# An attention and dynamic-filter kernel: score tiles of one and three banks in attention, and layer 1 without its split taps

## The chip, the cores and the metric

The kernel runs on one core of a Trainium2 chip. A core has five engines with instruction streams of their own: TensorE (PE, matmuls), VectorE (DVE), ScalarE (ACT), GpSimd (POOL) and SyncE (SP), and queues for transfers (DMA). They wait for each other through semaphores. The metric is the device time of one execution in microseconds. For the kernel before, it is the median of three runs.

## The reference, cut to what matters

Two layers work on `x` of shape (4, 256, 48, 48) in fp32. Layer 0 is a 3x3 convolution, then attention over all 2304 pixels with 8 heads of 32 channels. Layer 1 makes 45 weights for each pixel and uses them as five 3x3 filters with dilations 1, 6, 12, 24 and 36.

```python
# layer 0, after the convolution, its norm and relu
qkv = jnp.einsum('oc,bchw->bohw', qkv_w, x) + qkv_b[None, :, None, None]
q, k, v = (qkv[:, :, :d], qkv[:, :, d:2 * d], qkv[:, :, 2 * d:])      # per head, d = 32
attn = jax.nn.softmax(jnp.einsum('bhdn,bhdm->bhnm', q, k) * scale, axis=-1)
out = jnp.einsum('bhem,bhnm->bhen', v, attn).reshape(B, C, H, W)
out = jnp.einsum('oc,bchw->bohw', proj_w, out) + proj_b[None, :, None, None]
# layer 1
guidance = _conv(x, W_cat, pad=1)                                     # 45 channels
outs = [x]
for i, d in enumerate((1, 6, 12, 24, 36)):
    w = jax.nn.softmax(guidance[:, 9 * i:9 * (i + 1)], axis=1)
    outs.append(_dyn_branch(x, w, d))       # sum over 9 taps: shifted x times w[:, k]
y = _conv(jnp.concatenate(outs, axis=1), W_scale, pad=0)              # then a batch norm
# both layers: x = x + layer(group_norm(x))
```

## The kernel before

The images go through the core one after the other. Attention of image `b` stands alone. After it, layer 1 of image `b` runs together with the convolution and the q, k, v projections of image `b + 1`; after the last image, layer 1 stands alone, and the output is written.

**Attention.** The 2304 query columns of a group of four heads (there are two groups) are cut into units of 512 columns; eight units hold one group each, a ninth holds the last 256 columns of both. A unit goes through 18 key blocks `m` of 128 keys. A step is one block of one unit: four score matmuls, one for each head on its own 32 rows of the array, the exponential on ScalarE, then four matmuls that add the weighted values into `num`, and the sum of the exponentials over blocks (the divisor) on VectorE in `acc`. The order in the program is: scores of step i, then the weighted sums of step i - 1. PSUM has eight banks of 512 fp32 columns; three tiles of two banks hold scores, one bank holds `num`, one `den`.

```python
QC = 512
LENT = (2, 5, 8, 11, 14)
...
def ps2(name):
    return ps_s.tile([P, 2, 512], F32, tag="s", name=name)         # bufs=3

def scores(u, m):
    ss = [ps2(f"se_{b}_{u}_{m}_{pair}") for pair in range(2)]
    for g, q0, n, at in units[u]:
        for j, r in enumerate(heads):
            nc.tensor.matmul(ss[j // 2][:, j % 2, at : at + n],
                             k_[r, g, m * P : (m + 1) * P], q[r, g, q0 : q0 + n], ...)
    p = work0.tile([P, 4, QC], F32, tag="p", name=f"p_{b}_{u}_{m}", bufs=4)
    for pair in range(2):
        nc.scalar.activation(p[:, 2 * pair : 2 * pair + 2, :], ss[pair], AF.Exp, scale=QS)
    return p
```

For the five blocks in `LENT`, VectorE adds two of the four heads only; the other two are added by a transfer from GpSimd's queue that sums into `extra` in SBUF. After the last block `num` is copied out by ScalarE, so that its bank is free. `close` makes the divisor of a unit: it sums `acc` (and first `extra`) over the keys by a matmul with ones, takes the reciprocal by way of two transposes, and multiplies. `project` applies the output projection to 384 finished columns.

```python
def weigh(u, m, p):
    ...                                    # four matmuls p x vT into num
    if m == NT - 1:
        nc.vector.tensor_tensor(st["acc"][:, 2:], st["acc"][:, 2:], extra, ALU.add)
    ...
    js = slice(0, 2 if m in LENT else 4)
    nc.vector.tensor_tensor(st["acc"][:, js], other[:, js], p[:, js], ALU.add)
    if m == LENT[0]:
        nc.gpsimd.dma_start(out=extra, in_=p[:, 2:])
    elif m in LENT:
        nc.gpsimd.dma_start(out=extra, in_=p[:, 2:], accum_op=ALU.add)
    ...
    elif m == NT - 1:
        st["out"] = out
        nc.scalar.copy(out, st["num"])

for i, (u, m) in enumerate(steps):
    ps = scores(u, m)
    if prev is not None:
        weigh(*steps[i - 1], prev)
    prev = ps
    if m == 2 and u:
        close(u - 1)
    if m == 6 and u % NH == 0:
        ...                                # project finished chunks, in a ps2 tile
    if m > 2 and u > 1 and spare:
        spare.pop(0)(ps_a)                 # pieces of the next image's normalization
```

**Layer 1.** For each tap, a matmul (or a transfer and a copy) spreads the weight of a pixel over 128 partitions (`wb`), VectorE multiplies it with the shifted image, and GpSimd adds the product into `cat`; the sums then go through the output matmuls (`py`). The program's order is decided as it is built: a `clock` with estimated durations of each engine says which matmuls of layer 1 and of the next image's convolution come when. Some taps of the last image skip GpSimd: their products go straight into matmuls (`single`). Where GpSimd is behind by more than `SPLIT` on that clock, a tap in the first ones of a filter is split: VectorE multiplies both halves and adds one of them, and GpSimd adds only the other.

```python
split = (at > 0 and mine and not single
         and clock.t["POOL"] + added > clock.t["DVE"] + SPLIT)
mine = at == 0 or split or (mine and single)
...
elif split:
    nc.vector.tensor_tensor(pv, pw, src[:, 0], ALU.mult)
    nc.vector.tensor_tensor(pw, pw, src[:, 1], ALU.mult)
    dst = catv[:, 1, l0:l1, x0:x1]
    nc.vector.tensor_tensor(dst, dst, pw, ALU.add)
    dst = catv[:, 0, l0:l1, x0:x1]
    nc.gpsimd.tensor_tensor(dst, dst, pv, ALU.add)
```

Of the kernel before, what the change touches and what calls it, by code (L numbers as in the profile page):

```python
# [32 lines left out]

QC = 512
SAFE = 60.0
LENT = (2, 5, 8, 11, 14)
CATS = 4
PRODS = 5
SLACK = 3000.0
SPLIT = 4500.0  # L40
BEHIND = 0.0


# [5 lines left out]
def conv_preact_kernel(  # L49
# [482 lines left out]
    with tc.tile_pool(name="w", bufs=1) as wpool, tc.tile_pool(  # L532
# [394 lines left out]
        def attention(b, q, k_, vT, pools, spare, project, scratch):  # L927
# [6 lines left out]
            out = scratch[:, :QC]  # L934

            extra = scratch[:, QC : 3 * QC].rearrange("p (j n) -> p j n", j=2)
# [5 lines left out]
            assert NH * rest == QC  # L942
            heads = [slice(j * D, (j + 1) * D) for j in range(4)]

            def ps2(name):
                return ps_s.tile([P, 2, 512], F32, tag="s", name=name)

            def scores(u, m):
                ss = [ps2(f"se_{b}_{u}_{m}_{pair}") for pair in range(2)]
                for g, q0, n, at in units[u]:  # L950
                    for j, r in enumerate(heads):
                        nc.tensor.matmul(  # L952
                            ss[j // 2][:, j % 2, at : at + n],
                            k_[r, g, m * P : (m + 1) * P],
                            q[r, g, q0 : q0 + n],
                            start=True,
                            stop=True,
                        )
                p = work0.tile([P, 4, QC], F32, tag="p", name=f"p_{b}_{u}_{m}", bufs=4)
                for pair in range(2):  # L960
                    nc.scalar.activation(  # L961
                        p[:, 2 * pair : 2 * pair + 2, :], ss[pair], AF.Exp, scale=QS
                    )
                return p

            state = {}

            def weigh(u, m, p):
                if m == 0:
                    state[u] = dict(  # L970
                        num=ps_a.tile([P, 512], F32, tag="num", name=f"num_{b}_{u}"),
                        acc=work0.tile([P, 4, QC], F32, tag="acc", name=f"acc_{b}_{u}"),
                    )
                st = state[u]
                several = len(units[u]) > 1
                if several and m == 0:

                    for j, r in enumerate(heads):
                        nc.tensor.matmul(st["num"][r, :], zeros, p[:, j, :], start=True, stop=False)
                for i, (g, q0, n, at) in enumerate(units[u]):  # L980
                    for j, r in enumerate(heads):
                        nc.tensor.matmul(  # L982
                            st["num"][r, at : at + n],
                            vT[:, m, g * P + j * D : g * P + (j + 1) * D],
                            p[:, j, at : at + n],
                            start=(m == 0 and not several),
                            stop=(m == NT - 1 and i == len(units[u]) - 1),
                        )
                end = u == len(units) - 1
                if m == NT - 1:  # L990
                    nc.vector.tensor_tensor(st["acc"][:, 2:], st["acc"][:, 2:], extra, ALU.add)
                if end and m == NT - 1:
                    sums(u, p, True, False)
                elif m == 0:
                    st["first"] = p
                else:
                    other = st["first"] if m == 1 else st["acc"]
# [3 lines that stand above are left out]
                        nc.gpsimd.dma_start(out=extra, in_=p[:, 2:])  # L1001
                    elif m in LENT:
                        nc.gpsimd.dma_start(out=extra, in_=p[:, 2:], accum_op=ALU.add)  # L1003
                if end:
                    st["out"] = st["num"]
                elif m == NT - 1:
                    st["out"] = out
                    nc.scalar.copy(out, st["num"])  # L1008

            def sums(u, rhs, start, stop):  # L1010
                if start:
                    state[u]["den"] = ps_a.tile([P, 512], F32, tag="den", name=f"den_{b}_{u}")
                for j, r in enumerate(heads):
                    nc.tensor.matmul(
                        state[u]["den"][r, :], ones, rhs[:, j, :], start=start, stop=stop
# [1 line left out]

            def close(u):

                sums(u, state[u]["acc"], u < len(units) - 1, True)  # L1020
                st = state.pop(u)
                t = scratch
                nc.vector.transpose(t, st["den"])
# [4 lines left out]
                    rc.unsqueeze(2).to_broadcast([P, QC // D, D]),  # L1028
                )
                for g, q0, n, at in units[u]:  # L1030
                    nc.vector.tensor_tensor(
                        ao[:, g, q0 : q0 + n], st["out"][:, at : at + n], t[:, at : at + n],
                        ALU.mult,
                    )

            steps = [(u, m) for u in range(len(units)) for m in range(NT)]
            prev = None
            chunk = 0
            for i, (u, m) in enumerate(steps):
                ps = scores(u, m)  # L1040
                if prev is not None:
                    weigh(*steps[i - 1], prev)
                prev = ps
                if m == 2 and u:
                    close(u - 1)
                if m == 6 and u % NH == 0:
                    while (chunk + 1) * CH <= units[u][0][1]:
                        project(chunk, ao, ps2(f"pp_{b}_{chunk}"))
                        chunk += 1
                if m > 2 and u > 1 and spare:  # L1050
                    spare.pop(0)(ps_a)
            while spare:
                spare.pop(0)(ps_a)
            weigh(*steps[-1], prev)
            close(len(units) - 1)
            return ao, chunk

        def project(b, c, ao, pp, norm):
# [42 lines left out]
        def dynamic_filters(b, ao, chunk, norm, other, pools):  # L1101
# [241 lines left out]
            for c in range(NCK):  # L1343
# [21 lines left out]
                for j, (n, at, (k, oy, ox, y0, y1, x0, x1)) in enumerate(taps):  # L1365
# [18 lines left out]
                    else:  # L1384
# [25 lines left out]
                    split = (  # L1410
                        at > 0 and mine and not single
                        and clock.t["POOL"] + added > clock.t["DVE"] + SPLIT
                    )
                    mine = at == 0 or split or (mine and single)
                    if at == 0:
                        nc.vector.tensor_tensor(catv, wb, src, ALU.mult)  # L1416
                        end = summed = clock("DVE", ns, given)
                    elif split:
                        prod = work1.tile(
                            [P, NH, CH], F32, tag="prod", name=f"prod_{b}_{c}_{k}", bufs=PRODS  # L1420
                        )
                        pv = prod[:, 0, : nr * ncol].rearrange("p (r w) -> p r w", w=ncol)
                        pw = wb[:, 0]
                        nc.vector.tensor_tensor(pv, pw, src[:, 0], ALU.mult)
                        first = clock("DVE", half, given, slot("prod", PRODS))
                        nc.vector.tensor_tensor(pw, pw, src[:, 1], ALU.mult)
                        dst = catv[:, 1, l0:l1, x0:x1]
                        nc.vector.tensor_tensor(dst, dst, pw, ALU.add)
                        end = clock("DVE", 2 * half)
                        dst = catv[:, 0, l0:l1, x0:x1]  # L1430
                        nc.gpsimd.tensor_tensor(dst, dst, pv, ALU.add)
                        summed = max(clock("POOL", added / 2 + 90, first), end)
                        free["prod"].append(clock.t["POOL"])
                    else:
                        if single:
                            mixed("single", 2 * NH)
# [10 lines left out]
                    if single:  # L1447
                        for o in range(NH):
# [8 lines left out]
                    elif at and not split:  # L1457
                        dst = catv[:, :, l0:l1, x0:x1]
                        nc.gpsimd.tensor_tensor(dst, dst, pv, ALU.add)  # L1459
                        summed = clock("POOL", added, end)  # L1460
# [108 lines left out]
        for b in range(B + 1):  # L1569
# [130 lines left out]
            if b + 1 < B:  # L1700
# [1 line left out]
                u_next = taken(ORDER[0])  # L1702
                fin = [None]

                def step(ps_a, nn=nn, fin=fin, b=b):
                    if fin[0] is None:
                        fin[0] = nn.finish(
                            lambda name: ps_a.tile([P, 512], F32, tag="den", name=name)
                        )
                    if next(fin[0], fin) is fin:  # L1710
                        nn.shift_of()

                def piece(h, r0, b=b, nn=nn):
                    t = inside(pads[(b + 1) % 2], h, r0, R)
                    return lambda ps_a: nc.scalar.activation(
                        t, t, AF.Identity, bias=nn.shift[:, h : h + 1], scale=nn.rstd[:, h : h + 1]
                    )

# [3 lines left out]
            norm1 = Norm("n1", b)  # L1722
            q, k_, vT = qkv[b]
            with tc.tile_pool(name=f"work0_{b}", bufs=2) as work0, tc.tile_pool(
                name=f"ps_s_{b}", bufs=3, space=PSUM
            ) as ps_s, tc.tile_pool(name=f"ps_a_{b}", bufs=1, space=PSUM) as ps_a:
                ao, chunk = attention(
                    b, q, k_, vT, (ps_s, ps_a, work0), [f for _, f in spare],
# [77 lines left out]
```

## Time and profile before

| What | Value |
|---|---|
| median of three runs | 2929.42 us |
| range of the runs | 2926.9 to 2933.61 us |
| span of the profiled execution | 2927.6 us |
| mean granted clock of TensorE | 0.982 |
| exponentials (ScalarE) | 1296, mean 1027 ns, 1260.0 us |
| score matmuls, weighted sums (instructions) | 5760 and 5760 |
| adds into `acc` (VectorE) | 572, mean 1955 ns |
| summing transfers (GpSimd's queue) | 180, 4.5 us from issue to landing |
| adds into `cat` (GpSimd), whole and half | 661 and 81 |

The profile gives the busy time of each engine, groups of instructions by program line (with busy time, mean duration, and the idle time just before them with what ended it), and a timeline. Each fp32 matmul of the program appears as two instructions. A share of busy time says what an engine does, and not what it waits for: a PE whose matmul has begun and waits in the middle of a group counts as busy. So the stages have to be looked at apart, and within a stage, the steps.

### The profile page before, as it was taken

The page shows a single profiled execution, that of the slowest core. Times are in us where ns is not written, and L with a number is a line of the kernel's source. Part 1 is how long each engine was busy: PE and PEld are TensorE (multiplying, and loading weights), DVE is VectorE, ACT ScalarE, POOL GpSimd, SP SyncE. Part 2 cuts the span into 40 slices and gives each one's busy share as a digit, 9 for nine tenths or more (in the row PEclk, how much of TensorE's full clock was granted, in tenths as well). Part 3 has the DMA queues.
Part 4 walks back from the last instruction along what each step waited for, and adds up shares of the span by engine and source line. Part 5 has one row for each costly group of instructions (what it writes and reads, how often), then busy time and mean ns, then how long its engine had stood idle before and what let it go on. Part 6 is the DMA issues. An engine that isn't in the chain of part 4 may idle for free. (4 is left out here: it accounts for less than half of the span.)

```text
span 2927.6 us, 43833 instructions
## 1 busy us (share of the span) xinstructions
PE 2773.1 (95%) x16950; PEld 1246.7 (43%) x16950; DVE 2426.1 (83%) x2574; ACT 1675.2 (57%) x2104; POOL 1205.2 (41%) x1024
## 2 busy tenths in 40 slices
PE   7999999999999999999899999999999999998994
PEld 5622223556542222456562222355555222244562
DVE  6388999789868899778986899978886999986886
ACT  3489888322348988712236988852233888871224
POOL 1010010898840010299791100059986010005894
PEclk9999999999999999999999999999999999998997
DMA  4432333132252233323225333322213333335225
GB/s 179 100 69 64 67 76 71 53 87 86 73 127 62 61 78 69 68 65 95 69 68 124 71 69 69 68 63 76 82 50 85 69 75 67 71 67 218 54 74 204
DMA packets 146233, 244.64 MB, mean 84 GB/s; under 512 B 60952, under 2 KB 111968, under 8 KB 144224
## 3 DMA queue, kind: packets, MB, share of 16 engines
q0 software_dynamic: 26720, 99.79, 15.4%
q1 hardware_dynamic: 76960, 87.31, 10.4%
q10 hardware_dynamic: 42336, 54.66, 7.2%
q8 instruction: 135, 2.21, 0.3%
q14 instruction: 82, 0.67, 0.1%
HBM read 115.02 MB, written 32.33 MB: 50 GB/s over the span
## 5 line engine op out<-in xcount | busy, mean ns | idle before, releaser
L961 ACT ACTIVATE p<-se 128x1024 f32<-128x1024 f32 x1296 | 1260.0, 1027 | 239.7 <-PE se L952 171.2
L999 DVE TENSOR_TENSOR acc<-acc,p 128x2048 f32<-128x2048 f32 (+1 forms) x572 | 1118.4, 1955 | 101.2 <-ACT p L961 55.0
L1459 POOL TENSOR_TENSOR cat<-cat,prod 128x752 f32<-128x752 f32 (+9 forms) x661 | 883.1, 1345 | 133.6 <-DVE prod L1442 96.7
L952 PE MATMUL se<-q,k 32*128 32x512 f32 (+1 forms) x5760 | 819.6, 596 | 12.5 <-ACT p L961 6.2
L982 PE MATMUL num<-p,vT 128*32 128x512 f32 (+1 forms) x5760 | 699.0, 565 | 9.0 <-ACT scratch L1008 7.4
L1442 DVE TENSOR_TENSOR prod<-wb,pad 128x384 f32<-128x384 f32 (+8 forms) x687 | 483.4, 738 | 94.4 <-POOL cat L1459 55.9
L952 PEld LDWEIGHTS se<-q,k 32*128 32x128 f32 x5760 | 299.2, 184 | 533.6 <-issue 368.5
L1003 POOL DMA_DIRECT2D scratch<-p x144 | 122.6, 852 | 922.1 <-ACT p L961 872.9
L1281 PE MATMUL py<-cat,wsc 128*128 128x384 f32 x960 | 349.9, 494 | 9.8 <-POOL cat L1459 8.3
L1382 ACT COPY wb<-ws 128x384 f32<-128x384 f32 (+3 forms) x260 | 121.7, 468 | 371.1 <-DVE prod L1442 237.0
L982 PEld LDWEIGHTS num<-p,vT 128*32 128x32 f32 x5760 | 122.3, 108 | 491.2 <-issue 443.0
L1385 PE MATMUL wb<-w,pick 128*128 128x384 f32 (+3 forms) x628 | 299.7, 509 | 24.7 <-DVE prod L1442 15.8
L1281 PEld LDWEIGHTS py<-cat,wsc 128*128 128x128 f32 x960 | 176.3, 192 | 114.8 <-POOL cat L1459 24.8
L1001 POOL DMA_DIRECT2D scratch<-p x36 | 20.1, 558 | 467.8 <-DVE acc L999 339.2
L1385 PEld LDWEIGHTS wb<-w,pick 128*128 128x128 f32 x628 | 116.5, 190 | 140.2 <-DVE prod L1442 63.4
L851 PE MATMUL pc<-cv_q,u 128*128 128x288 f32 x576 | 160.9, 413 | 7.0 <-DVE cv_q L742 6.2
L1133 PE MATMUL pg<-pad,wcat 128*45 128x384 f32 x864 | 158.4, 498 | 1.6 <-DVE pad L592 1.4
L851 PE MATMUL pc<-cv_k,u 128*128 128x288 f32 x576 | 155.0, 407 | 3.3 <-DVE yt L786 1.8
L884 PE MATMUL pq<-hid,wqkv 128*128 128x384 f32 x384 | 135.5, 492 | 11.8 <-DVE yt L786 11.8
L851 PEld LDWEIGHTS pc<-cv_q,u 128*128 128x128 f32 x576 | 108.3, 192 | 37.3 <-DVE cv_q L742 6.3
L1416 DVE TENSOR_TENSOR cat<-wb,pad 128x768 f32<-128x768 f32 x120 | 114.0, 950 | 11.4 <-PE wb L1385 10.8
L851 PEld LDWEIGHTS pc<-cv_k,u 128*128 128x128 f32 x576 | 106.6, 189 | 32.5 <-DVE yt L786 2.5
(221 smaller groups left out, 1976.4 us busy)
## 6 DMA issues: line engine op xcount, KB each, us to landing
scratch<-p POOLq DMA_DIRECT2D x180, 512.0 KB, 4.5
ws<-w_d ACTq DMA_DIRECT2D x256, 192.0 KB, 3.2
pad<-in_x SPq DMA_DIRECT2D x14, 1152.0 KB, 15.6
u<-u_d SPq DMA_DIRECT2D x18, 768.0 KB, 4.7
x_d<-pad SPq DMA_DIRECT2D x48, 192.0 KB, 2.5
xst<-in_x SPq DMA_DIRECT2D x36, 192.0 KB, 2.4
y_d<-y SPq DMA_DIRECT2D x18, 384.0 KB, 3.4
u_d<-u SPq DMA_DIRECT2D x6, 768.0 KB, 3.7
```

The lines of the kernel that those rows point to most:

```text
L851: nc.tensor.matmul(m, u[:, h, kx, o * P : (o + 1) * P], halves[g][:, h, i, :, kx : kx + WW], start=(h == 0 and kx == 0), stop=(h == NH - 1 ...
L884: nc.tensor.matmul(pq[:, :CH], wqkv[:, i, s, g * P : (g + 1) * P], hid[:, i, cols], start=(i == 0), stop=(i == NH - 1),)
L952: nc.tensor.matmul(ss[j // 2][:, j % 2, at : at + n], k_[r, g, m * P : (m + 1) * P], q[r, g, q0 : q0 + n], start=True, stop=True,)
L961: nc.scalar.activation(p[:, 2 * pair : 2 * pair + 2, :], ss[pair], AF.Exp, scale=QS)
L982: nc.tensor.matmul(st["num"][r, at : at + n], vT[:, m, g * P + j * D : g * P + (j + 1) * D], p[:, j, at : at + n], start=(m == 0 and not s ...
L999: nc.vector.tensor_tensor(st["acc"][:, js], other[:, js], p[:, js], ALU.add)
L1003: nc.gpsimd.dma_start(out=extra, in_=p[:, 2:], accum_op=ALU.add)
L1133: nc.tensor.matmul(pg[64 * s : 64 * s + NG, :CH], wcat[:, ii, k, :], window(gn, ii, cc * R, k // 3 - 1, k % 3 - 1), start=(i == 0 and k == 0),
L1281: nc.tensor.matmul(to, wsc[:, n * NH + i, o * P : (o + 1) * P], rhs(i), start=(n == 0 and i == 0), stop=(last and i == NH - 1),)
L1385: nc.tensor.matmul(pw[:, : nr * WW], pick[:, k : k + 1].to_broadcast([P, P]), w[:, l0 * WW : l1 * WW], start=True, stop=True,)
L1442: nc.vector.tensor_tensor(pv, wb, src, ALU.mult)
L1459: nc.gpsimd.tensor_tensor(dst, dst, pv, ALU.add)
```

## The change

In attention:

- Scores of head 0 go into a tile of one bank (one buffer), those of heads 1 to 3 into a tile of three banks (two buffers). With `num`, these are all eight banks. The exponential is taken in 512 and 1536 columns. The aim is that the scores of a step need not wait for the exponentials of the step just before.
- The bank for `den` is gone. The divisor of a unit takes its turn among the three-bank tiles, as do the projection and the statistics of the next image's norm. It is made two units later, ahead of the weighted sums, so that a turn of the tiles comes where PE has other work.
- Six key blocks are summed by transfers instead of five. The sum with `extra` comes after the unit's last add. `num` is copied straight into `ao`, where it is multiplied in place.

In layer 1 the split taps are gone, and with them `SPLIT`; the estimated duration of GpSimd's adds for 36 columns and fewer is 110 ns shorter than in the kernel before.

The diff, cut to its core:

```diff
-LENT = (2, 5, 8, 11, 14)
+LENT = (2, 5, 8, 10, 13, 15)
-SPLIT = 4500.0
...
-            def ps2(name):
-                return ps_s.tile([P, 2, 512], F32, tag="s", name=name)
+            def three(name):
+                return ps_s.tile([P, 3, 512], F32, tag="s", name=name)     # bufs=2

             def scores(u, m):
-                ss = [ps2(f"se_{b}_{u}_{m}_{pair}") for pair in range(2)]
+                s1, s3 = ps_a.tile([P, 512], F32, tag="one", ...), three(f"se_{b}_{u}_{m}")
...
+                        dst = s3[:, j - 1] if j else s1
...
-                for pair in range(2):
-                    nc.scalar.activation(
-                        p[:, 2 * pair : 2 * pair + 2, :], ss[pair], AF.Exp, scale=QS
-                    )
+                nc.scalar.activation(p[:, 0, :], s1, AF.Exp, scale=QS)
+                nc.scalar.activation(p[:, 1:, :], s3, AF.Exp, scale=QS)
...
-                if m == NT - 1:
-                    nc.vector.tensor_tensor(st["acc"][:, 2:], st["acc"][:, 2:], extra, ALU.add)
...
+                if m == NT - 1:
+                    rest = st["acc"][:, 2:]
+                    nc.vector.tensor_tensor(rest, rest, extra, ALU.add)
+                    if not end:
+                        g, q0, n, _ = units[u][0]
+                        nc.scalar.copy(ao[:, g, q0 : q0 + n], st["num"])
...
-                    state[u]["den"] = ps_a.tile([P, 512], F32, tag="den", name=f"den_{b}_{u}")
+                    state[u]["den"] = three(f"den_{b}_{u}")[:, 0, :]
...
                 ps = scores(u, m)
+                if m == 1 and u > 1:
+                    close(u - 2)
                 if prev is not None:
                     weigh(*steps[i - 1], prev)
                 prev = ps
-                if m == 2 and u:
+                if m == 2 and u == last:
                     close(u - 1)
-                if m == 6 and u % NH == 0:
-                    while (chunk + 1) * CH <= units[u][0][1]:
-                        project(chunk, ao, ps2(f"pp_{b}_{chunk}"))
+                if m == 6 and (u % NH == 1 or u == last):
+                    while (chunk + 1) * CH <= units[u if u == last else u - 1][0][1]:
+                        project(chunk, ao, three(f"pp_{b}_{chunk}"))
...
-                    half = 0.525 * ns + 150
-                    ns, added = 1.05 * ns + 150, 2.1 * ns + (80 if 36 < ncol < WW else 190)
+                    ns, added = 1.05 * ns + 150, 2.1 * ns + (190 if ncol == WW else 80)
...
-                    split = (
-                        at > 0 and mine and not single
-                        and clock.t["POOL"] + added > clock.t["DVE"] + SPLIT
-                    )
-                    mine = at == 0 or split or (mine and single)
...                  (the split branch, shown above, is taken out)
```

More of the change, by code (lines that the diff above doesn't have):

```diff
@@ L933, in attention @@
             nc.gpsimd.memset(zeros, 0.0)
-            out = scratch[:, :QC]
-            extra = scratch[:, QC : 3 * QC].rearrange("p (j n) -> p j n", j=2)
+            extra = scratch[:, : 2 * QC].rearrange("p (j n) -> p j n", j=2)
             scratch = work0.tile([P, QC], F32, tag="rt", name=f"rt_{b}", bufs=1)
@@ L943, in attention @@
             heads = [slice(j * D, (j + 1) * D) for j in range(4)]
-            def ps2(name):
-                return ps_s.tile([P, 2, 512], F32, tag="s", name=name)
+            def three(name):
+                return ps_s.tile([P, 3, 512], F32, tag="s", name=name)
             def scores(u, m):
-                ss = [ps2(f"se_{b}_{u}_{m}_{pair}") for pair in range(2)]
+                s1, s3 = ps_a.tile([P, 512], F32, tag="one", name=f"so_{b}_{u}_{m}"), three(f"se_{b}_{u}_{m}")
                 for g, q0, n, at in units[u]:
                     for j, r in enumerate(heads):
+                        dst = s3[:, j - 1] if j else s1
                         nc.tensor.matmul(
-                            ss[j // 2][:, j % 2, at : at + n],
+                            dst[:, at : at + n],
                             k_[r, g, m * P : (m + 1) * P],
@@ L959, in scores @@
                 p = work0.tile([P, 4, QC], F32, tag="p", name=f"p_{b}_{u}_{m}", bufs=4)
-                for pair in range(2):
-                    nc.scalar.activation(
-                        p[:, 2 * pair : 2 * pair + 2, :], ss[pair], AF.Exp, scale=QS
-                    )
+                nc.scalar.activation(p[:, 0, :], s1, AF.Exp, scale=QS)
+                nc.scalar.activation(p[:, 1:, :], s3, AF.Exp, scale=QS)
                 return p
             state = {}
+            last = len(units) - 1
             def weigh(u, m, p):
@@ L988, in weigh @@
                         )
-                end = u == len(units) - 1
-                if m == NT - 1:
-                    nc.vector.tensor_tensor(st["acc"][:, 2:], st["acc"][:, 2:], extra, ALU.add)
+                end = u == last
                 if end and m == NT - 1:
@@ L1003, in weigh @@
                         nc.gpsimd.dma_start(out=extra, in_=p[:, 2:], accum_op=ALU.add)
[L1004 to L1008, printed above, removed]
+                if m == NT - 1:
[4 more added lines that the diff above has]
+                        nc.scalar.copy(ao[:, g, q0 : q0 + n], st["num"])
             def sums(u, rhs, start, stop):
                 if start:
-                    state[u]["den"] = ps_a.tile([P, 512], F32, tag="den", name=f"den_{b}_{u}")
+                    state[u]["den"] = three(f"den_{b}_{u}")[:, 0, :]
                 for j, r in enumerate(heads):
@@ L1018, in close @@
             def close(u):
-                sums(u, state[u]["acc"], u < len(units) - 1, True)
+                sums(u, state[u]["acc"], u < last, True)
                 st = state.pop(u)
@@ L1030, in close @@
                 for g, q0, n, at in units[u]:
-                    nc.vector.tensor_tensor(
-                        ao[:, g, q0 : q0 + n], st["out"][:, at : at + n], t[:, at : at + n],
-                        ALU.mult,
-                    )
+                    dst = ao[:, g, q0 : q0 + n]
+                    src = dst if u < last else st["num"][:, at : at + n]
+                    nc.vector.tensor_tensor(dst, src, t[:, at : at + n], ALU.mult)
             steps = [(u, m) for u in range(len(units)) for m in range(NT)]
@@ L1043, in attention @@
                 prev = ps
-                if m == 2 and u:
+                if m == 2 and u == last:
                     close(u - 1)
-                if m == 6 and u % NH == 0:
-                    while (chunk + 1) * CH <= units[u][0][1]:
-                        project(chunk, ao, ps2(f"pp_{b}_{chunk}"))
+                if m == 6 and (u % NH == 1 or u == last):
+                    while (chunk + 1) * CH <= units[u if u == last else u - 1][0][1]:
+                        project(chunk, ao, three(f"pp_{b}_{chunk}"))
                         chunk += 1
                 if m > 2 and u > 1 and spare:
-                    spare.pop(0)(ps_a)
+                    spare.pop(0)(three)
             while spare:
-                spare.pop(0)(ps_a)
+                spare.pop(0)(three)
             weigh(*steps[-1], prev)
-            close(len(units) - 1)
+            close(last)
             return ao, chunk
@@ L1407, in dynamic_filters @@
                     )
-                    split = (
-                        at > 0 and mine and not single
-                        and clock.t["POOL"] + added > clock.t["DVE"] + SPLIT
-                    )
-                    mine = at == 0 or split or (mine and single)
                     if at == 0:
@@ L1417, in dynamic_filters @@
                         end = summed = clock("DVE", ns, given)
[L1418 to L1433, printed above, removed]
                     else:
@@ L1456, in dynamic_filters @@
                             ))
-                    elif at and not split:
+                    elif at:
                         dst = catv[:, :, l0:l1, x0:x1]
@@ L1703, in conv_preact_kernel, with step @@
                 fin = [None]
-                def step(ps_a, nn=nn, fin=fin, b=b):
+                def step(three, nn=nn, fin=fin, b=b):
                     if fin[0] is None:
-                        fin[0] = nn.finish(
-                            lambda name: ps_a.tile([P, 512], F32, tag="den", name=name)
-                        )
+                        fin[0] = nn.finish(lambda name: three(name)[:, 0, :])
                     if next(fin[0], fin) is fin:
@@ L1714, in piece @@
                     t = inside(pads[(b + 1) % 2], h, r0, R)
-                    return lambda ps_a: nc.scalar.activation(
+                    return lambda three: nc.scalar.activation(
                         t, t, AF.Identity, bias=nn.shift[:, h : h + 1], scale=nn.rstd[:, h : h + 1]
@@ L1724, in conv_preact_kernel @@
             with tc.tile_pool(name=f"work0_{b}", bufs=2) as work0, tc.tile_pool(
-                name=f"ps_s_{b}", bufs=3, space=PSUM
+                name=f"ps_s_{b}", bufs=2, space=PSUM
             ) as ps_s, tc.tile_pool(name=f"ps_a_{b}", bufs=1, space=PSUM) as ps_a:
```

## The prediction

> **What bounds the kernel now.** I read the page first, then a table of the span in stretches, then the timeline of one attention stage. The page gives PE the largest share:
>
> ```profile
> PE 2773.1 (95%) x16950; PEld 1246.7 (43%) x16950; DVE 2426.1 (83%) x2574; ACT 1675.2 (57%) x2104; POOL 1205.2 (41%) x1024
> ```
>
> The table by stage shows that the mix differs. The kernel alternates attention (second and fourth rows here) with layer 1 of one image beside the convolution of the next (third row); after the stretch and its length, the columns are the busy us of PE, weight loads, VectorE, ScalarE and GpSimd, with instructions, then PE's clock, the DMA share and GB/s.
>
> ```profile
> 143.00:522.00 379.00, 375.90 (x2998) 115.52 (x3002) 339.69 (x219) 327.17 (x351) 35.61 (x45) 1.00 0.32 69
> 522.00:846.00 324.00, 304.65 (x1213) 186.54 (x1207) 257.32 (x406) 86.22 (x170) 282.69 (x217) 0.98 0.27 74
> 846.00:1230.00 384.00, 378.78 (x2992) 115.41 (x2986) 340.18 (x218) 324.58 (x350) 35.72 (x45) 0.99 0.37 80
> ```
>
> In attention PE reads 99% busy, but a matmul that waits half way through a group still counts, so I looked at single steps. A step is 8 score matmuls and 8 weighted sums. From the timeline:
>
> ```profile
> 305.33 1.06 PE L982 MATMUL num<-p,vT 128*32 128x512 f32 x8
> 306.32 1.14 PE L952 MATMUL se<-q,k 32*128 32x512 f32 x8
> 307.39 1.06 PE L982 MATMUL num<-p,vT 128*32 128x512 f32 x8
> 307.50 1.94 ACT L961 ACTIVATE p<-se 128x1024 f32<-128x1024 f32 x2 [0.30 <-PE se L952]
> 308.39 0.48 PEld L952 LDWEIGHTS se<-q,k 32*128 32x128 f32 x8 [0.84 <-PE se L952]
> 308.39 1.31 PE L952 MATMUL se<-q,k 32*128 32x512 f32 x8
> 309.63 1.06 PE L982 MATMUL num<-p,vT 128*32 128x512 f32 x8
> ```
>
> From score start to score start one step takes 2.07 us (306.32 to 308.39) and the next 2.23. In the longer one the scores last 1.31 us instead of 1.14, and their weight loads 0.48. Its second pair of banks is the one that the first exponential (from 307.50) is still reading: three two-bank tiles serve two pairs a step, so pair 1 of a step reuses the tile of pair 0 of the step before. ScalarE in turn waits 0.30 us for scores. So neither engine is simply full; they hold each other up through that tile. All 161 intervals of the first image add up to 375 us.
>
> At the start of a unit of 18 steps two more things appear:
>
> ```profile
> 311.44 0.59 ACT L1008 COPY scratch<-num 128x512 f32<-128x512 f32 x1
> 312.08 1.06 PE L982 MATMUL num<-p,vT 128*32 128x512 f32 x8 [0.27 <-ACT scratch L1008]
> 315.03 1.04 PE L1014 MATMUL den<-acc,ones 128*32 128x512 f32 x8
> ```
>
> The sums of the new unit wait for the copy of the old one (its step takes 2.45 us), and the divisors add 0.86 us of PE work (2.93).
>
> **What the skill says.** (1) The Trainium skill, "ScalarE: Activation LUTs", section "What ACT_TABLE_LOAD costs": an activation with immediate scale and bias costs 186 ns plus 0.833 ns a column, and neighbours overlap by about 93 ns. The trace has 1027 ns for 1024 columns (the formula: 1039), and 1.94 us for two, an overlap of 0.11. So 512 + 1536 columns should cost ScalarE what 1024 + 1024 do. (2) "TensorEngine Tiling (Array Packing)", "Gotcha 1: PSUM Pressure": different row tiles write to different PSUM banks. The four heads here are four row tiles, each with a bank in both kernels, so the matmuls need not change. (3) "GPSIMD Engine Reference", section 3.1: a two-input add takes 1.96 times VectorE's time. Here it is 1523 ns against about 848 for 672 elements, a ratio of 1.8. (4) "DMA: Bandwidth & Descriptors", "Anatomy of one DMA": about 2 us of a GpSimd transfer are fixed, mostly completion. The trace has 4.5 us from issue to landing for a summing transfer of 512 KB.
>
> **Part 1, the score banks.** Head 0 gets one bank, heads 1 to 3 a tile of three, two of these. Head 0 of the next step then waits only for a 512-column exponential, about 0.60 us (the 512-column copy above is 0.59), which ends well inside the 1.03 us of sums that PE does first. The tile of three has a whole step. So each 2.23 us step should become 2.07. PE's own work per image: 161 x 2.07 = 333, eight divisors x 0.86 = 7, five projection chunks inside attention x 2.8 = 14 (the steps with a chunk take 4.85 to 5.07), one group of zeros 1: 355 us, 20 under the present 375.
>
> Not all 20 come. Twelve steps with a slice of the next image's normalization take 2.42 us because ScalarE is full there (0.35 x 12 = 4, stays). A divisor now takes one of two score tiles, so the following scores must reuse the tile whose 1536-column exponential is still running, queued behind the copy: scores end at T, the copy runs to about T+0.5, the exponentials to T+2.5, while PE would be ready at T+1.95. That is 0.6 us in 7 units, 4 us; on the other hand, the divisor hides the wait for the copy. Two statistics matmuls (tiles too) about 1 us each, chunks some 2 in all: 12 left of the 20. Gain about 8 us an image, **30 us** in four.
>
> **Part 2, six blocks by transfer.** The page has:
>
> ```profile
> L999 DVE TENSOR_TENSOR acc<-acc,p 128x2048 f32<-128x2048 f32 x392 | 898.1, 2291 | 80.9 <-ACT p L961 49.1 <-DVE acc L999 0.5
> L999 DVE TENSOR_TENSOR acc<-acc,p 128x1024 f32<-128x1024 f32 x180 | 220.3, 1224 | 20.3 <-ACT p L961 5.9
> L1003 POOL DMA_DIRECT2D scratch<-p x144 | 122.6, 852 | 922.1 <-ACT p L961 872.9
> ```
>
> A unit costs VectorE 12 x 2.29 + 6 x 1.22 + 2.4 for closing = 37.2 us now, against 40 us a unit. With PE at about 38.7 that would be tight, as the chunks add 1.3 a unit. The sixth block takes off 1.07: 36.1. So this gives nothing by itself; it keeps VectorE from becoming the bound. Its price: blocks 8 and 10, 13 and 15 are two steps (4.1 us) apart, less than a summing transfer takes (4.5), so the later one waits on GpSimd and keeps its `p` buffer, one of four, about 6 us. The buffer is due back after about 6.3. I allow 0.12 us a unit, 4 us in all, and 2 more where the input images load at the start of attention in two images. Attention: 30 - 6 = **24 us less**.
>
> **Part 3, layer 1 without its split.** A split tap has three half-size VectorE operations and one half-size GpSimd add:
>
> ```profile
> L1426 DVE TENSOR_TENSOR wb<-wb,pad 128x336 f32<-128x336 f32 x44 | 22.2, 505 | 0.0
> L1431 POOL TENSOR_TENSOR cat<-cat,prod 128x336 f32<-128x336 f32 x44 | 36.9, 838 | 2.2
> L1442 DVE TENSOR_TENSOR prod<-wb,pad 128x672 f32<-128x672 f32 x92 | 76.5, 848 | 3.9 <-POOL cat L1459 3.5 <-ACT wb L1382 0.4
> L1459 POOL TENSOR_TENSOR cat<-cat,prod 128x672 f32<-128x672 f32 x87 | 132.5, 1523 | 8.8 <-DVE prod L1442 2.5
> ```
>
> Whole again, a tap gives VectorE back 3 x 0.50 - 0.85 = 0.66 us and costs GpSimd 1.52 - 0.84 = 0.69. There are 81 of them, 20 or 21 a stage: GpSimd gets 14 us more per stage. Its busy time in the third row above leaves 41 us of 324, but most of that lies from 700 to 760 us, where VectorE makes convolution outputs. Taps delayed before that have room to catch up; 7 of the first stage's 20 lie after 760, where GpSimd runs without gaps to the end. These are 7 x 0.69 = 4.8 us at the end of a stage, of which convolution matmuls can fill some: 4 us in three stages. In the last stage GpSimd is full nearly throughout. There the schedule turns two more taps into matmuls (28 instead of 26), and I take 4 us. Layer 1: **16 us more**.
>
> The sum: 2929.4 - 24 + 16 = 2921; I lean a little to the attention side, since the waits that I left in may overlap each other, and say 2918.
>
> **Rivals.** (a) The two-tile ring is worse than the three-tile one: a divisor, chunk or statistic takes half of it, and each may cost a whole exponential (1.5 us). There are 36 + 20 + 6 such uses; at 1.5 us each that is 93 us, more than the 4 x 20 = 80 that Part 1 could give at best: with Part 3 about 2958. Against it: the divisor's own PE time covers most of the exponential. (b) The split was worth little, as GpSimd has gaps: then only attention counts, 2900 to 2905. For it speaks that PE is 94% busy in the third row, and that VectorE gets 13 us a stage back. (c) The transfers become the bound: if each of the 72 close pairs holds ScalarE for 0.5 us instead of my 4 us in all, 36 us come back, and the time is about 2953. Against it: at present ScalarE waits on these transfers only three times, while images load.
>
> **Range and chances.** Attention can give 5 to 45 us, layer 1 can cost 3 to 30. Taken as independent: 2890 to 2944. For 2% faster (below 2871), nearly PE's whole floor would have to be met with nothing lost in layer 1: 0.04. For 2% slower (above 2988), rivals (a) and (c) would both have to hold: 0.02.
>
> **What would show it.** Right: score steps all near 2.07 us, no weight loads of 0.48 in plain steps, a unit near 38.7; the attention stages some 6 us shorter each, the layer 1 stages some 4 us longer, with more PE waits for GpSimd's `cat`. Wrong: waits of ScalarE for the transfers in every unit; steps after a divisor above 4 us; layer 1 stages unchanged.

## The result, and the profile after

The changed kernel takes 2942.85 us (median of four runs, 2937.97 to 2944.82); the kernel before, in the same session, 2929.01. The ratio is 1.0043, with a 95% interval of 1.0025 to 1.006. It is slower by 0.4%. The forecast of 2918 had the sign wrong, and the time lies 1 us inside the upper end of the range (2890 to 2944).

The first part of the page, after:

```profile
PE 2754.2 (94%) x16967; PEld 1204.1 (41%) x16967; DVE 2352.2 (80%) x2412; ACT 1673.7 (57%) x2103; POOL 1286.8 (44%) x1058
```

PE's busy time fell by 19 us and VectorE's by 74, yet the span grew from 2927.6 to 2943.0. GpSimd alone has more to do (1205.2 before): its adds into `cat` take 48.5 us longer, summed over the trace, and 31 us are the issuing of the additional transfers. The table of stretches, cut at the stage bounds of this run, says where that counts. The first and third row are attention of two images, the second is layer 1 beside a convolution, as in the prediction's table (whose text counts its rows one too high); the columns are those of that table.

```profile
143.00:511.00 368.00, 365.75 (x2954) 102.49 (x2958) 326.71 (x217) 323.59 (x348) 42.68 (x54) 1.00 0.38 82
511.00:844.00 333.00, 307.43 (x1235) 188.01 (x1229) 252.88 (x368) 86.08 (x169) 296.22 (x217) 0.98 0.25 69
844.00:1229.00 385.00, 373.00 (x2950) 103.66 (x2950) 327.50 (x218) 322.71 (x348) 43.45 (x55) 0.98 0.44 94
```

For a comparison I took, from the timelines of both kernels, the first and the last step's score start of each image. The attention stretches and what lies between them:

| | before | after | difference |
|---|---|---|---|
| attention, images 1 to 4 | 375.0, 384.9, 384.5, 374.9 | 367.8, 385.1, 378.6, 361.0 | -26.8 us |
| last score start to next attention, or to the end | 322.2, 322.2, 318.2, 302.5 | 333.5, 332.7, 327.8, 313.7 | +42.6 us |

The second line of the table begins with the end of attention, the last divisor, which takes 7 us longer in all than before (see last_unit_five). So attention gave about 20 us (24 were forecast), and layer 1 took about 35 instead of 16.

Plain steps in attention are now even. From the timeline after:

```profile
286.06 0.69 PE L953 MATMUL so<-q,k 32*128 32x512 f32 x1
286.06 0.70 PE L953 MATMUL se<-q,k 32*128 32x512 f32 x3
286.59 0.59 PE L953 MATMUL so<-q,k 32*128 32x512 f32 x1
286.60 0.60 PE L953 MATMUL se<-q,k 32*128 32x512 f32 x3
287.13 1.07 PE L982 MATMUL num<-p,vT 128*32 128x512 f32 x8
287.21 0.60 ACT L961 ACTIVATE p<-so 128x512 f32<-128x512 f32 x1
287.71 1.45 ACT L962 ACTIVATE p<-se 128x1536 f32<-128x1536 f32 x1
288.13 0.69 PE L953 MATMUL so<-q,k 32*128 32x512 f32 x1
```

The scores start at 286.06, 288.13 and, further on, 290.19: 2.07 us each time. The exponential of head 0 ends at 287.81, before PE comes to the next scores at 288.13, so nothing waits in the middle of a group. ScalarE's two exponentials, 0.60 and 1.45 us with an overlap of 0.10, take 1.95, as two equal ones did (1.94).

The waits show the other side. Columns are the line that waited, for whom, the total us, how often, and the longest. Before, then after:

```profile
DVE prod L1442 <- POOL cat L1459: 55.9, 77, 1.6
POOL cat L1459 <- DVE prod L1442: 96.7, 41, 37.9
```

```profile
DVE prod L1420 <- POOL cat L1437: 142.1, 194, 1.6
POOL cat L1437 <- DVE prod L1420: 84.9, 31, 36.4
```

VectorE waits for GpSimd to free a product buffer 86 us longer, although it has less work. GpSimd's own idle time before the adds shrank by 12 us only, though the adds take 48.5 us longer; some 36 us of it are in both kernels a single wait ahead of the last stage. It could use hardly any of the room that the prediction gave it.

### The profile page after: what moved, and what is told of

The parts are those of the page before. It is cut to its first block, busy times and chain, and to the rows that moved or that the text cites. A ratio compares the mean times of both kernels' runs of the same rounds, so it can differ in the third digit from the quotient of the medians.

```text
span 2943.0 us, 43553 instructions
## 1 busy us (share of the span) xinstructions
PE 2754.2 (94%) x16967; PEld 1204.1 (41%) x16967; DVE 2352.2 (80%) x2412; ACT 1673.7 (57%) x2103; POOL 1286.8 (44%) x1058
## 5 line engine op out<-in xcount | busy, mean ns | idle before, releaser
L997 DVE TENSOR_TENSOR acc<-acc,p 128x2048 f32<-128x2048 f32 (+1 forms) x572 | 1080.2, 1888 | 122.7 <-ACT p L962 76.1
L1437 POOL TENSOR_TENSOR cat<-cat,prod 128x752 f32<-128x752 f32 (+7 forms) x740 | 996.4, 1357 | 125.7 <-DVE prod L1420 84.9
L962 ACT ACTIVATE p<-se 128x1536 f32<-128x1536 f32 x648 | 942.6, 1455 | 3.1 <-PE se L953 3.1
L953 PE MATMUL so<-q,k 32*128 32x512 f32 (+1 forms) x1440 | 733.6, 597 | 28.6 <-ACT p L961 21.8
L953 PE MATMUL se<-q,k 32*128 32x512 f32 (+1 forms) x4320 | 742.5, 597 | 0.4 <-ACT p L962 0.4
L1420 DVE TENSOR_TENSOR prod<-wb,pad 128x768 f32<-128x768 f32 (+7 forms) x768 | 552.8, 747 | 183.6 <-POOL cat L1437 142.1
L1001 POOL DMA_DIRECT2D scratch<-p x180 | 153.7, 854 | 972.2 <-ACT p L962 598.5
L961 ACT ACTIVATE p<-so 128x512 f32<-128x512 f32 x648 | 392.1, 605 | 210.3 <-PE se L953 95.6
L953 PEld LDWEIGHTS so<-q,k 32*128 32x128 f32 x1440 | 217.9, 184 | 545.8 <-ACT p L961 494.0
L953 PEld LDWEIGHTS se<-q,k 32*128 32x128 f32 x4320 | 228.5, 184 | 9.6 <-ACT p L962 7.0
L999 POOL DMA_DIRECT2D scratch<-p x36 | 20.1, 558 | 371.9 <-ACT p L962 322.0
```

The costliest lines, as they stand in the source:

```text
L953: nc.tensor.matmul(dst[:, at : at + n], k_[r, g, m * P : (m + 1) * P], q[r, g, q0 : q0 + n], start=True, stop=True,)
L961: nc.scalar.activation(p[:, 0, :], s1, AF.Exp, scale=QS)
L962: nc.scalar.activation(p[:, 1:, :], s3, AF.Exp, scale=QS)
L1420: nc.vector.tensor_tensor(pv, wb, src, ALU.mult)
```

## The experiments

Each is compared with the kernel before by runs on the same chip. Shown are the ratio with its 95% interval and the median.

**attn_only.** The changed kernel with layer 1 put back.

```diff
+SPLIT = 4500.0
...
+                    split = (at > 0 and mine and not single
+                             and clock.t["POOL"] + added > clock.t["DVE"] + SPLIT)
...                  (and the split branch and the estimate of the kernel before)
```

> Attention of the changed kernel, layer 1 of the kernel before, splits included. Theory A (attention gave about 27 us, as its score steps show, and layer 1 took about 42): 2929 - 27 = 2902 us, between 2897 and 2908. Rival B (the two sides depend on each other: the new attention leaves the next stage in a worse position, so part of the 42 us belongs to it): above 2912 us, with layer 1 stages that stay longer than 325 us though the splits are back.

Measured: 0.9919 (0.9903 to 0.9936), 2907.35 us. Some 24 us faster, near theory A's 27, within its bounds (by 1 us). VectorE's waits for GpSimd are back at 52.7 us, and what lies between the attention stages at 320 to 324. Rival B falls.

**layer1_only.** Attention of the kernel before, without the split branch, and with the estimate of the changed kernel.

> Attention of the kernel before, layer 1 of the changed kernel. Theory A: the whole loss of about 42 us is here, so 2929 + 42 = 2971 us, between 2965 and 2977. Rival B: less than 2962 us.

Measured: 1.0109 (1.0093 to 1.0126), 2966.07 us: 27 to 37 us slower. That is at the lower edge of theory A's range, with a kernel before that took 2931.94 in this comparison. The two sides together, -24 and +32, make +8; the change itself measured +13, so they add up within the intervals. Theory A's 42 is too large; 7 us of it, as will be seen, came from the end of attention.

**layer1_old_estimate.** The kernel before without the split branch, and with its own estimate.

```diff
-                    split = (...)
...
                     ns, added = 1.05 * ns + 150, 2.1 * ns + (80 if 36 < ncol < WW else 190)
```

> The kernel before with only its split taken out; the longer estimate for GpSimd's adds of 36 and fewer columns stays. Theory C (the loss is GpSimd's own work: 14 us a stage on an engine that is full): as in the run with both sides of layer 1 changed, 2971 us within 5. Rival D (a good part comes from the shorter estimate, which makes the built order expect GpSimd's sums too early and PE wait for them): clearly less, 2950 to 2960 us.

Measured: 1.0111 (1.0094 to 1.0128), 2965.49 us, the same as with the other estimate (and half a microsecond under theory C's bounds). Rival D falls: the estimate costs nothing that can be measured, the missing splits all.

**no_early_splits** and **no_late_splits.** Here the prediction's step is tested: that taps delayed early in a stage catch up later. The 20 taps that the kernel before splits are listed, and a part is left whole.

```diff
+SPLIT_AT = {(0, 9), (0, 10), (1, 9), ... (5, 28)}        # (chunk, tap), 20 of them
...
+                    if not alone:
+                        split = (c, k) in SPLIT_AT and c >= 4     # no_early_splits
+                        split = (c, k) in SPLIT_AT and c < 4      # no_late_splits
```

> The kernel before, with the 13 splits of the first three row chunks taken out in each of the three stages that overlap with a convolution (39 taps, 13 x about 0.66 = 8.5 us of GpSimd a stage); the 7 of the last two chunks that have any, and the last stage, stay. Theory G (the prediction's: an early delay is caught up where GpSimd waits for VectorE's convolution outputs): at most 4 us more than before. Theory H (GpSimd's backlog is limited by the five product buffers, so VectorE waits too and everything after is late): 3 x 7 to 8.5, 20 to 26 us more than before.

Measured: 1.0034 (1.002 to 1.0049), 2944.62 us: 6 to 14 us slower, between the two theories. GpSimd's adds take 23 us longer (26 had been expected); of these about 10 reach the end of the kernel, and not 0 to 4. The early delay is caught up only in part.

> The kernel before, with the 7 splits of the last chunks taken out in each of the three stages that overlap with a convolution (21 taps, 4.7 us of GpSimd a stage); the early 13 and the last stage stay. Both theories: 8 to 14 us more than before, as GpSimd runs without gaps to the end of the stage.

Measured: 1.0031 (1.0019 to 1.0044), 2941.87 us: about 9 us slower, for 14 us of GpSimd work. As expected. The waits of VectorE in the two:

```profile
DVE prod L1449 <- POOL cat L1466: 101.3, 146, 1.4
```

```profile
DVE prod L1449 <- POOL cat L1466: 100.3, 137, 1.6
```

Each half of the splits costs VectorE some 45 us of waiting more than before (55.9). What lies beneath: a tap passes from VectorE to GpSimd in one of five product buffers, so GpSimd can be behind by five adds at most. In the trace of the changed kernel, 155 of VectorE's 159 waits of this kind in the three stages beside a convolution end with four earlier products still to be added: the fifth buffer has just come free. During such a wait VectorE does nothing, and the convolution outputs that stand behind the tap in its program can't go ahead of it. The time from 690 to 750 us, where GpSimd has room, is hardly filled with what was left over. From 690 us on, before:

```profile
690.00:720.00 30.00, 26.94 (x103) 18.53 (x102) 29.77 (x36) 7.83 (x14) 25.67 (x16) 1.00 0.22 68
720.00:750.00 30.00, 24.57 (x81) 15.43 (x80) 25.34 (x38) 9.19 (x18) 18.31 (x15) 0.94 0.28 69
```

And after, with the stretches around:

```profile
660.00:690.00 30.00, 28.40 (x105) 18.46 (x104) 25.30 (x40) 4.77 (x10) 27.17 (x21) 1.00 0.30 96
690.00:720.00 30.00, 25.84 (x95) 17.91 (x93) 29.51 (x34) 7.64 (x14) 25.91 (x16) 0.94 0.27 70
720.00:750.00 30.00, 26.04 (x83) 16.64 (x83) 24.09 (x39) 9.18 (x17) 19.75 (x16) 0.89 0.30 70
750.00:780.00 30.00, 29.83 (x100) 17.99 (x98) 27.33 (x41) 11.55 (x22) 27.27 (x17) 1.00 0.25 74
```

GpSimd (the fifth pair) was idle for 16.0 us in these 60 us before and is still for 14.3, while the stretch ahead of them runs it at 27 of 30.

That the number of buffers sets the loss is read from these waits, and not shown by a run: **three_products**, the kernel before without splits and with three product buffers instead of five, deadlocked and gave no time.

**split_3000** and **split_2000.** The other direction: more splits, on the changed attention with five blocks by transfer (attn_five, below, 2897.67 us).

```diff
-SPLIT = 4500.0
+SPLIT = 3000.0        # 140 taps split instead of 81; 2000.0: 186
```

> The changed attention with five blocks by transfer and the splits in layer 1 (2898 us), with the bound for a split at 3000 ns instead of 4500: 140 taps are split instead of 81. Theory H (GpSimd paces layer 1 wherever it is behind; leaving out 81 splits cost 34 us, 0.42 us a split): the next 59 give back something, but less each, as VectorE gets 0.66 us for each: 8 to 20 us less, 2878 to 2890. Theory K (81 took what there was to take, VectorE is now as full as GpSimd): 2898 within 5.

Measured: 0.9862 (0.9843 to 0.9881), 2893.26 us.

> The same with the bound at 2000 ns: 186 taps split. Theory H: 2870 to 2892, at most a little below the run with 3000, since GpSimd has then lost 105 x 0.69 = 72 us and VectorE gained 69 over the run with 4500, and VectorE becomes the fuller of the two. Theory K: more than 2898.

Measured: 0.9863 (0.9845 to 0.9882), 2892.94 us. Both are just outside of what theory H said (2890 at most, and 2892 at most). Theory K's 2898 within 5 holds for the first, its "more than 2898" fails for the second. They are some 5 us below attn_five, and all three intervals overlap, so that even these 5 us are not sure. The waits tell more. With 3000, then with 2000:

```profile
DVE prod L1445 <- POOL cat L1462: 19.5, 21, 3.2
POOL cat L1462 <- DVE prod L1445: 121.0, 69, 37.4
```

```profile
DVE prod L1445 <- POOL cat L1462: 3.4, 5, 1.5
POOL cat L1462 <- DVE prod L1445: 151.8, 105, 40.1
```

With 81 splits VectorE waited 55.0 us for GpSimd and GpSimd 94.3 for VectorE. With 186 it is 3.4 and 151.8: now GpSimd waits for VectorE. The 81 took nearly all that there was to take; 59 more bring about 5 us at most, and the next 46 nothing.

**attn_five.** As attn_only, with five blocks.

```diff
-LENT = (2, 5, 8, 10, 13, 15)
+LENT = (2, 5, 8, 11, 14)
```

> As the run with the changed attention alone, but with five key blocks summed by transfers (2, 5, 8, 11, 14) as before. Theory E (the sixth block gives nothing by itself, since a unit costs VectorE 37.2 us against PE's 38.6; its close pairs cost waits while the input images load): the same time or up to 6 us less. Rival F (VectorE at 37.2 and chunks 1.3 a unit is too near to 38.6, so that it becomes the bound): 5 to 20 us more, with ScalarE waiting for VectorE's adds.

Measured: 0.9885 (0.9869 to 0.9902), 2897.67 us, 10 us less than with six. ScalarE's waits for VectorE's adds are 4.5 us in all (0.9 in attn_only), so rival F falls, and the sixth block is a loss, a little larger than theory E said. The summing transfers in the profile after are seen waiting for each other, 212.2 us on GpSimd's queue (35.3 before, 72.7 in attn_five):

```profile
L1001 POOL DMA_DIRECT2D scratch<-p x180 | 153.7, 854 | 972.2 <-ACT p L962 598.5 <-DMA scratch<-p 212.2 <-ACT p L961 157.2
```

**last_unit_five.** Six blocks, but five in the last unit of an image.

```diff
+LENT_LAST = (2, 5, 8, 11, 14)
...
+                    lent = LENT_LAST if end else LENT
-                    js = slice(0, 2 if m in LENT else 4)
+                    js = slice(0, 2 if m in lent else 4)
```

> The changed attention with the splits in layer 1 (2907 us with six blocks by transfer in every unit, 2898 with five), six blocks in all units but the last of an image, which takes five (2, 5, 8, 11, 14). Theory I (six cost time only at the end of an image, where blocks 13 and 15 are close together and the last divisor waits for the last transfer, about 2 us in four images): 2898 us within 4. Rival J (the transfers cost in all units, or in the units while images load): 2903 us or more.

Measured: 0.9886 (0.987 to 0.9903), 2900.21 us, theory I's value within its bounds. At an image's end nothing is left to do beside the last divisor, so a late transfer shows. The sum with `extra` at the end of the second image in attn_only:

```profile
1213.09 0.85 POOL L1002 DMA_DIRECT2D scratch<-p  x1 [4.12 <-DMA scratch<-p]
1218.41 2.06 DVE L1005 TENSOR_TENSOR acc<-acc,scratch 128x1024 f32<-128x1024 f32 x1 [2.31 <-DMA scratch<-p]
1220.53 1.05 PE L1014 MATMUL den<-acc,ones 128*32 128x512 f32 x4 [1.86 <-DVE acc L1005]
```

GpSimd's queue issues the transfer of block 15 only when that of block 13 has landed (it stands for 4.12 us, and the landing ends that). VectorE stands for 2.31 us until block 15 has landed too, and then the divisor's matmuls wait 1.86 us for VectorE, whose sum takes 2.06 us here (1.22 at the same place in attn_five; why is not shown). From the last step's score start to the end of the divisor's matmuls, the four images take 7.2, 8.8, 8.8 and 7.2 us in attn_only, 7.0, 7.0, 7.0 and 6.7 in attn_five, and 7.1, 7.4, 8.8 and 8.6 in the changed kernel (before: 6.1, 6.4, 6.1, 6.1). Between attn_only and attn_five that is 4 us of the 7 to 10. The rest lies in layer 1 stages by up to 2 us each, and I can't say why.

**late_load**, **act_load** and **act_load_3000.** The first units of the second and third image take 46.9 and 47.9 us in the changed kernel, against 38.6 in the first image and 39.8 in the fourth. In both, two input images are loaded at that time; in the fourth it is one, and in the first both have landed before attention starts. I tried to move one of the loads.

```diff
-                load_pad(b + 1)
+                if b:
+                    later.append(lambda b=b: load_pad(b + 1))
...
                 ps = scores(u, m)
+                if u == 1 and m == 0 and later:
+                    later.pop()()
```

> The changed attention with five blocks and the splits (2898 us), but in the second and third image the input of the image after the next stage is loaded at the start of the second unit of attention, not at the start of the first. Theory L (in these two images the first unit is some 9 us longer than in the first image because the summing transfers share the DMA engines with two image loads): 6 to 14 us less, 2884 to 2892, with first units near 42 us. Rival M (the load disturbs the second unit as much): 2898 within 4.

Measured: 0.9893 (0.9874 to 0.9912), 2902.07 us; first units 46.7 and 47.2 us. This told nothing, since SyncE had nothing to wait for at the new place and ran ahead: the load only changed places with the next one of its queue (it starts at 849.95 us instead of 841.67 in attn_five). In the next runs ScalarE's queue issues it.

> As the run with the late load (2902 us), whose load in fact started only 8 us later: SyncE's queue runs ahead of the other engines. Here ScalarE's queue issues it, so that it comes after the exponentials of the first unit. Theory L: the first units of the second and third image fall from 46.4 and 47.9 us to 38 to 42, and the time from 2898 to 2884 to 2892. Rival M: the second unit gets longer by as much, 2898 within 4.

Measured: 0.9912 (0.9895 to 0.9929), 2907.17 us. The first units fall to 41.0 us each, as theory L says, and ScalarE's waits for summing transfers in them from 4.2 and 6.5 to 3.1 and 1.3 us: the image load does slow these transfers. But the second units rise from 37.7 to 45.1. The timeline of ScalarE's queue in act_load:

```profile
876.57 0.66 ACTq L1696 DMA_DIRECT2D pad<-in_x  x1
877.27 5.93 ACTq L1696 DMA_DIRECT2D pad<-in_x  x1
```

The second half of the load holds ScalarE for 5.93 us, and one step takes 8.34. So the loss is moved and not removed, as rival M has it, if by another cause; the time, some 8 us above attn_five, is over what both had said.

> The same with the bound for splits at 3000 (2893 us with the load where it was). Theory L and theory H together: 2880 to 2888. Rival M: 2893 within 4.

Measured: 0.9873 (0.9857 to 0.9889), 2896.05 us, no better than without the move, as rival M had it. The fastest version of the study stays the changed attention with five blocks and the bound at 3000 or 2000: 2893 us, 1.4% below the kernel before.

## Why the prediction was right in part

- *Scores, 2.23 to 2.07 us:* right. All plain steps measure 2.06 to 2.08 us.
- *A divisor takes a tile and costs 0.6 us, but hides the copy:* right, here 0.45 us. Timeline after, at the start of a unit:

```profile
268.56 1.06 PE L1013 MATMUL den<-acc,ones 128*32 128x512 f32 x8 [0.20 <-ACT p L962]
269.16 1.66 ACT L962 ACTIVATE p<-se 128x1536 f32<-128x1536 f32 x1
269.44 1.04 PE L982 MATMUL num<-p,vT 128*32 128x512 f32 x8
270.42 0.69 PE L953 MATMUL so<-q,k 32*128 32x512 f32 x1
270.87 0.31 PEld L953 LDWEIGHTS se<-q,k 32*128 32x128 f32 x6 [0.17 <-ACT p L962]
270.87 0.70 PE L953 MATMUL se<-q,k 32*128 32x512 f32 x3
```

  Head 0 starts at 270.42, heads 1 to 3 wait until 270.87 for their tile: 0.45 us. A plain unit takes 38.6 us; 38.7 was said.
- *Attention 30 us faster, less 6 for transfers:* -26.8 in the profiles, about -20 with the late end of attention, and -24 in the run of its own. The parts differ: the fourth image, which has no next image to load or normalize for, gained 13.9 us, and the second nothing (it takes 385.1 us; 378.8 in attn_only). Apart from the sixth block, no run takes the edits in attention one by one: that the score banks gave the gain is read from the steps. ScalarE's waits for the summing transfers are 25.4 us (8.2 before), 17 more instead of 6.
- *The sixth block keeps VectorE from becoming the bound:* wrong. With five, ScalarE waits 4 us more for VectorE's adds; with six, 10 us are lost. I had worked out a margin of 0.2 us a unit (37.2 + 1.3 against 38.7), and read it as none. The late landing at an image's end (4 us) was not in the sum at all.
- *Layer 1 costs 4 us a stage, "Taps delayed before that have room to catch up":* this is the step that failed. The work was sized about rightly (GpSimd's adds take 12.4 us longer in a stage; 14 was said), but the stages are 9.6 to 11.3 us longer, of which 1.0 to 2.8 are the end of attention. In the runs, early taps cost about 10 us in all instead of nothing, late ones 9 against 12; the last stage cost about 8 against 4 in the profile of layer1_only. These make 27 of the 32 us, and the rest is no larger than the intervals. In the profiles, what lies between the attention stages is, over three stages, 15.5 us longer without the early splits, 12.9 without the late ones and 30.7 without both: the halves nearly add up. The idle time of GpSimd that I counted as room comes where VectorE makes the convolution's outputs or waits for them, and five buffers carry little work over to it.

That the time still lies inside the range is owed to attention, and is luck as far as layer 1 goes: its 32 us (27 to 37) are more than the 3 to 30 that the prediction allowed it.

The three rivals of the prediction all failed to show. The two-tile ring costs about what was said, the close transfers held GpSimd's queue, but ScalarE only 19 times (25.4 us in all, not 36), and the split was worth more and not less.

## What to carry to other kernels

When two engines pass work on through a few buffers, idle time of the second one while the first is busy elsewhere is only in part a reserve for it: the backlog can't be larger than the buffers. Here about 10 of 23 us of work that was delayed early reached the end. Look at the waits in both directions before shifting work between them; what the receiver waits for and what the sender waits for tell which one paces, and how much a shift can still bring. And a transfer that is hidden inside a loop shows at the end of it, where nothing is left beside it: choose the last turn's timing by itself.

## What the runs showed of the hardware that had not been expected

A load of half an image (1152 KB) issued from ScalarE's queue right after the first half held ScalarE for 5.93 us, where the first took 0.66. This is not ScalarE's own: the same pair issued by SyncE in the kernel before, at 107 us, took 0.66 and 6.16. And a later place in the program of SyncE moved a load by only some 8 us: a queue with nothing to wait for runs ahead of the other engines.
